# Splitting the first exponential of an attention step and the wide products beside it

## The chip, the cores and the metric

The kernel runs on one core of a Trainium2 chip. A core has five engines that run their own instruction streams and wait for each other through semaphores: TensorE (PE in the profile, with its weight loads shown apart as PEld), VectorE (DVE), ScalarE (ACT), GpSimd (POOL) and SyncE (SP), which here issues the DMA transfers. TensorE writes its results into PSUM, a memory of 128 partitions with eight banks of 512 fp32 columns each. VectorE and ScalarE read the results from there.

The metric is the time of one execution in device microseconds, as the median of several runs. One further execution is taken with the hardware profiler, and all the rows below come from it.

## The reference

The input is x of shape (8, 1024, 256): eight sequences of 1024 tokens. Sixteen heads of 16 columns each attend causally. Everything is fp32.

```python
mod = (_silu(c) @ wmod).reshape(8, 6, 1, -1)          # shift, scale and gate, twice
h = _layernorm(x) * (1 + ca) + sa
x = x + ga * attention(h)       # softmax(q k / 4, causal) v, 16 heads of 16, then w_out, b_out
h = _layernorm(x) * (1 + cb) + sb
# channel mix: xr, xk are mixtures of h and of h one token earlier
x = x + gb * sigmoid(xr @ W_r) * (relu(xk @ W_k) ** 2 @ W_v)
```

## The kernel before

**Units and steps.** Attention is done in 32 units, one for each of 8 sequences and 4 groups of 4 heads. A unit's 1024 queries are two chunks of 512 columns (`CW`), and its 1024 keys are eight tiles of 128. The table `STEPS` cuts a unit into nine steps, `a` to `e` for the tiles on the causal diagonal and `0` to `3` for the full tiles below it. Each step fills 512 columns of four banks with scores. Step `a` has one part of 512 columns, step `c` two of 256, and steps `b` and `d` have one of 128 and one of 384, because a diagonal tile needs only the queries from it on.

**What a step issues.** The function `step` is called once for each step of the whole program. It interleaves two kinds of work of two different units, nine steps apart (`LAG`):

- *Weights* (`weights`) of the older unit: for each of the four heads three rounds of products (`q,k` twice, for the high and low part of q, and `m,ones`, which subtracts the maximum) go into one bank. Then four exponentials on ScalarE, one for each head, read a whole bank each and write the tile `w`. Two heads make a half. GpSimd then zeroes what lies above the diagonal.
- *Maxima* (`maxima`) of the newer unit: two rounds of products (`k,q`) go into two pairs of banks, and VectorE takes the largest value of each row, for a diagonal tile with a mask added in place.

All eight banks are taken: four for the weights and four for the maxima. The rounds of a step lie in two streams. Stream 0 has the weights of half 0 and then the maxima of half 0. Stream 1 has the maxima of half 1 and then the weights of half 1. The loop at the end of `step` takes the next round from the stream that has had fewer columns so far (`took`), and the product's own column count is what is added. TensorE's order is fixed by this: each of its instructions is tied to the one before it (`InOrder` with `always`).

**What fills the rest of a step.** After the two streams come the *fills* that tables such as `POST` and `PREP` place on each step: the q and k projections (`qk`), the v projection and the output projection (`rows`), transposes (`transposed`), and the channel mix (`receptance`, `key`, `multiplied`). After two to three steps' worth of weights, `attend` multiplies the exponentials with v into a bank `po`, at the end of the step after the last one it needs. `attend` also reads `w` and so waits for GpSimd on the diagonal steps.

**Which bank a fill gets.** The functions `bank` and `banks_of_step` keep, for each bank, an estimated time at which it will be free, and hand out the one that is free first. For the first fill of a step this is in nearly all steps the bank of the step's first exponential.

**Strips.** Outside a few steps `by_strips` issues a product of 128 rows as four products of 32 output rows, one for each quarter of the array's columns, which run side by side. In `rows` the moving operand is 256 columns wide; in `qk`, `key` and `attend` it is as wide as the bank, 512 columns. Each fp32 product appears twice in the trace, as two passes.

**The end.** When no unit is left for the maxima, the flag `late[0]` is set and stays set for the last nine steps.

The profile puts every instruction at line 160, the helper that records it, so rows are told apart by the tiles they write and read. All PSUM banks are one tile named `banks`.

Of the kernel before, what the change touches and what calls it, by code (L numbers as in the profile page):

```python
# [10 lines left out]
AF = mybir.ActivationFunctionType  # L11
# [4 lines left out]
P = 128  # L16
B, N, D = 8, 1024, 256
H, HD = 16, 16
DC = D // P
CW = 512  # L20
NC = N // CW
NT = CW // P
HG = 4
NG = H // HG
ST = 32
# [28 lines left out]
FIRST, LAST = ("a", "f", "g"), ("e", "h", "i")  # L54
LAG = 9
BANKS = 8
PIECES = {0: NT, 1: 2 * NT}


# [15 lines left out]
def adaln_block(  # L75
# [24 lines left out]

    vacant, here = [0.0] * BANKS, [0.0]

# [35 lines left out]
    late = [False]  # L138
# [9 lines left out]
    start = [False]  # L148
# [28 lines left out]
    pe, dve, act = InOrder(nc.tensor, True), InOrder(nc.vector), InOrder(nc.scalar)  # L177
# [78 lines left out]
    wk_sb = load(w_k, D, "wk_sb")  # L256
# [54 lines left out]
    def v_tile(b, i):  # L311
        return v_of[(b * NC + i // NT) % (2 * NC)][:, i % NT]
# [121 lines left out]
    def by_strips(to, lhs, rhs, start, stop):  # L434


        if wide[0]:
            pe.matmul(to, lhs, rhs, start=start, stop=stop)
            return
        for j in range(P // ST):  # L440
            of = slice(j * ST, (j + 1) * ST)
            pe.matmul(to[of, :], lhs[:, of], rhs, start=start, stop=stop)
# [11 lines left out]
                )  # L454


    def prep(b, c):
        S = A[b, c]

        def stats(*ts):  # L460
            statistics(S["xa"], S, f"a{b}_{c}", ts)

        def norm(half):
            normalise(S["xa"], S, f"a{b}_{c}", half)
            if half == 0:
                return
            nxt = b * NC + c + 1
            if 1 < nxt < B * NC:
                later(lambda: load_xa(nxt // NC, nxt % NC))

        def turn():
            S["hT"] = sb.tile([P, DC, CW], F32, tag="hT", bufs=2, name=f"hT{b}_{c}")
            for d in range(DC):
                name = f"pta{b}_{c}_{d}"
                transposed(S["h"], S["hT"][:, d, :], b, d, SHIFT_A, SCALE_A, name)

        def qk(n, half):

            pq = bank(f"pq{b}_{c}_{n}_{half}")
            at = n * D + half * P  # L480
            for d in range(DC):
                by_strips(
                    pq, wqk_sb[:, d, at : at + P], S["hT"][:, d, :], d == 0, d == DC - 1
                )
            w, hi = (
                sb.tile([P, CW], F32, tag="qk", bufs=4, name=f"qk{b}_{c}_{n}_{half}{h}")
                for h in range(2)
            )
            if n == 0:
                act.mul(w, pq, SCALE)  # L490
            else:
                act.copy(w, pq)
            hi, lo = hi.bitcast(F32R), w.bitcast(F32R)
            pool.tensor_copy(hi, w)
            pool.tensor_sub(lo, w, hi.bitcast(F32))

            def away():
                to = (q_in, k_in)[n][b % 2][half]
                for h, of in enumerate((hi, lo)):
                    sync.dma_start(to[:, h, c * CW : (c + 1) * CW], of.bitcast(F32))  # L500

            later(away)

        def v(t0):
            pv = bank(f"pv{b}_{c}_{t0}")
            rows(pv, S["hT"], wv_sb, (t0, t0 + 1))
            to = v_of[(b * NC + c) % (2 * NC)]
            act.copy(
                to[:, t0 : t0 + 2, : H * (HD + 1)].rearrange(
                    "p t (h e) -> p t h e", e=HD + 1  # L510
                )[:, :, :, :HD],
                pv.rearrange("p (t h e) -> p t h e", t=2, e=HD),
            )

        return dict(
            stats0=lambda: stats(0, 1),
            stats1=lambda: stats(2, 3),
            stat0=lambda: stats(0),
            stat1=lambda: stats(1),
            stat2=lambda: stats(2),  # L520
            stat3=lambda: stats(3),
            norm0=lambda: norm(0),
            norm1=lambda: norm(1),
            turn=turn,
            q0=lambda: qk(0, 0),
            k0=lambda: qk(1, 0),
            q1=lambda: qk(0, 1),
            k1=lambda: qk(1, 1),
            v0=lambda: v(0),
            v2=lambda: v(2),  # L530
        )
# [127 lines left out]
    def weights(u, k, half, pws):  # L659

        diagonal = STEPS[k][0][2]
        V = U[u]
        qs, kk = qs_of[u % KEPT], k_of[u % KEPT]
        js = (2 * half, 2 * half + 1)
        pw = pws[half]
        parts, total = parts_of(k)
        rounds = []
        for c, kt, lo, cols in parts:
            for h in range(3):

                def products(c=c, kt=kt, lo=lo, cols=cols, h=h):
                    for n2, j in enumerate(js):
                        at = j * ST
                        if h < 2:
                            rs = slice(at, at + ST)
                            left = kk[rs, kt * P : (kt + 1) * P]
                            right = qs[h][rs, c * CW + lo : (c + 1) * CW]
                        else:
                            left = ones[at : at + 2, :]
                            right = V["m", c][at : at + 2, lo:]  # L680
                        pe.matmul(pw[n2][:, cols], left, right, start=h == 0, stop=h == 2)

                rounds.append((CW - lo, products))

        def exponentials():
            w = sb.tile([P, 2, CW], F32, tag="w", bufs=8, name=f"w{u}_{k}_{half}")
            for n2 in range(2):
                act.activation(w[:, n2, :total], pw[n2][:, :total], AF.Exp)
            if diagonal:

                blocks = len(parts)
                apart = parts[-1][3].start or CW
                on = w.rearrange("p h (m q) -> p h m q", q=apart)[:, :, :blocks, :P]
                pool.affine_select(
                    out=on,
                    in_=on,
                    pattern=[[0, 2], [0, blocks], [1, P]],
                    compare_op=ALU.is_ge,
                    fill=0.0,
                    base=0,  # L700
                    channel_multiplier=-1,
                )
            V["w", k, half] = w

        return rounds, exponentials, 0
# [4 lines left out]
    def attend(u, k, then):  # L710

        c, steps, _ = groups_of(u)[k]
        V = U[u]
        b, g = divmod(u, NG)
        po = bank(f"po{u}_{k}")

        parts = sorted(
            ((at, *part[1:]) for at in steps for part in parts_of(at)[0] if part[0] == c),
            key=lambda part: part[2],
        )  # L720
        ws = {(at, half): V["w", at, half] for at in steps for half in range(2)}
        for m, (at, kt, lo, cols) in enumerate(parts):
            for j in range(HG):
                pe.matmul(
                    po[j * ST : (j + 1) * ST, lo:],
                    v_tile(b, kt)[:, (g * HG + j) * (HD + 1) :][:, :ST],
                    ws[at, j // 2][:, j % 2, cols],
                    start=m == 0,
                    stop=m == len(parts) - 1,
                )  # L730
        then()
        if ("o", c) not in V:
            V["o", c] = sb.tile([P, CW], F32, tag="o", bufs=3, name=f"o{u}_{c}")
            act.copy(V["o", c], po)
        elif strict[0]:
            more = sb.tile([P, CW], F32, tag="more", bufs=2, name=f"more{u}_{k}")
            act.copy(more, po)
            pool.tensor_add(V["o", c], V["o", c], more)
        else:
            dve.tensor_add(V["o", c], V["o", c], po)  # L740
# [88 lines left out]
    def post(b, c):  # L829
        S = A[b, c]  # L830
# [75 lines left out]

        def key(e):
            pk = bank_apart(f"pk{b}_{c}_{e}")
            for d in range(DC):
                by_strips(  # L910
                    pk, wk_sb[:, d, e * P : (e + 1) * P], S["step"][:, d, :], d == 0, d == DC - 1
                )
            if e == 0:
                S["ka"] = sb.tile([P, DC, CW], F32, tag="mix", bufs=2, name=f"ka{b}_{c}")
            ka = S["ka"][:, e, :]
            act.activation(ka, pk, AF.Relu)
            pool.tensor_mul(ka, ka, ka)
# [204 lines left out]
    def step(T, T1, S, now, fill):  # L1122
# [26 lines left out]
        while any(lists):  # L1149
            s = min((s for s in range(2) if lists[s]), key=lambda s: (took[s], lists[s][0][3], s))  # L1150
            cols, products, after, _ = lists[s].pop(0)
            took[s] += cols
            products()
            if after:
                after()
# [290 lines left out]
```

## Time and profile before

| | |
|---|---|
| Median of three runs | 1377.53 us (1376.43 to 1382.0) |
| Profiled execution | 1386.23 us, with a span of 1384.5 us from the first to the last instruction |
| TensorE busy | 1284.9 us, 93% of the span |
| VectorE busy | 1056.9 us, 76% |
| ScalarE busy | 861.5 us, 62% |
| GpSimd busy | 710.7 us, 51% |
| DMA | 106 GB/s on average |
| Granted TensorE clock | 0.961 of full speed on average |

The profiled execution took 8.7 us more than the median of the unprofiled runs. Its busy shares are averages over some 300 steps that repeat the same pattern of nine. A matmul's end is modelled in the trace, so starts are the safer numbers on TensorE.

### The profile page before, as it was taken

The page shows a single profiled execution, that of the slowest core. Times are in us where ns is not written, and L with a number is a line of the kernel's source. Part 1 is how long each engine was busy: PE and PEld are TensorE (multiplying, and loading weights), DVE is VectorE, ACT ScalarE, POOL GpSimd, SP SyncE. Part 2 cuts the span into 40 slices and gives each one's busy share as a digit, 9 for nine tenths or more (in the row PEclk, how much of TensorE's full clock was granted, in tenths as well). Part 3 has the DMA queues.
Part 4 walks back from the last instruction along what each step waited for, and adds up shares of the span by engine and source line. Part 5 has one row for each costly group of instructions (what it writes and reads, how often), then busy time and mean ns, then how long its engine had stood idle before and what let it go on. Part 6 is the DMA issues. An engine that isn't in the chain of part 4 may idle for free.

```text
span 1384.5 us, 41749 instructions
## 1 busy us (share of the span) xinstructions
PE 1284.9 (93%) x16570; PEld 692.5 (50%) x16570; DVE 1056.9 (76%) x2910; ACT 861.5 (62%) x1679; POOL 710.7 (51%) x1088
## 2 busy tenths in 40 slices
PE   7898999999999899998999899998999989999988
PEld 4354555544455445554455454554455544544546
DVE  5776777788777877778777888778878788778745
ACT  2475677757567566765666666675666656656562
POOL 1334646546355556455565555564644556555352
PEclk8998999999999999999999999999999999999999
DMA  5114434422344323332434213443223323220111
GB/s 164 68 55 140 163 117 134 147 91 71 106 156 132 96 89 111 132 113 94 129 125 145 92 64 125 149 139 98 85 93 132 133 95 114 95 93 31 51 36 35
DMA packets 86515, 146.70 MB, mean 106 GB/s; under 512 B 12200, under 2 KB 42792, under 8 KB 86320
## 3 DMA queue, kind: packets, MB, share of 16 engines
q1 hardware_dynamic: 86112, 143.84, 31.4%
q8 instruction: 130, 2.13, 0.6%
q14 instruction: 65, 0.53, 0.1%
q10 hardware_dynamic: 208, 0.20, 0.0%
HBM read 86.35 MB, written 56.08 MB: 103 GB/s over the span
## 4 chain that ended last, share of the span: by engine, by line
PE 66%; DVE 9%; POOL 8%; ACT 7%; issue 5%; DMA 0%; POOLq 0%; DVEq 0%; ACTq 0%; SPq 0%
PE banks L160 66%; DVE mix L160 4%; ACT w L160 3%; DVE max L160 2%; POOL qk L160 2%; ACT w_e L160 1%; DVE banks L160 1%; POOL o L160 1%; POOL xb L160 1%; ACT w_d L160 1%; POOL oT L160 1%; POOL w_c L160 1%; POOL w_b L160 1%; POOL mrow L160 1%; POOL w_a L160 0%
## 5 line engine op out<-in xcount | busy, mean ns | idle before, releaser
L160 DVE CUSTOM_DVE_ANT_0 banks<-banks,mask 128x256 f32<-128x256 f32 (+3 forms) x1024 | 467.0, 525 | 121.9 <-PE banks L160 119.4
L160 PE MATMUL banks<-k,q 32*128 32x512 f32 (+3 forms) x3072 | 427.3, 371 | 5.8 <-DVE k L160 3.7
L160 PE MATMUL banks<-q,k 32*128 32x512 f32 (+3 forms) x3072 | 398.1, 369 | 5.4 <-ACT hT L160 1.2
L160 DVE TENSOR_REDUCE max<-banks 128x2 f32<-128x1024 f32 x256 | 302.5, 1221 | 91.7 <-PE banks L160 91.5
L160 PEld LDWEIGHTS banks<-q,k 32*128 32x128 f32 x3072 | 236.5, 185 | 149.0 <-ACT w L160 43.5
L160 ACT ACTIVATE w<-banks 128x512 f32<-128x512 f32 x512 | 264.2, 603 | 61.7 <-PE banks L160 58.4
L160 PE MATMUL banks<-m,ones 2*128 2x512 f32 (+3 forms) x1536 | 262.0, 351 | 8.7 <-DMA m<-mrow 8.7
L160 PEld LDWEIGHTS banks<-k,q 32*128 32x128 f32 x3072 | 252.0, 185 | 29.9 <-DVE max L160 5.9
L160 PEld LDWEIGHTS banks<-m,ones 2*128 2x128 f32 x1536 | 144.7, 185 | 16.1 <-DMA m<-mrow 7.1
L160 DVE DVE_READ_ACCUMULATOR2_ANT max<- 128x1 f32 x1024 | 143.2, 140 | 0.0
L160 PE MATMUL banks<-hT,wqk_sb 128*32 128x512 f32 x960 | 117.6, 610 | 10.6 <-ACT w_b L160 5.0
L160 PE MATMUL banks<-w,v 128*32 128x512 f32 x1024 | 123.2, 599 | 0.4 <-ACT w_a L160 0.2
L160 POOL TENSOR_TENSOR o<-o,more 128x512 f32<-128x512 f32 x62 | 79.2, 1277 | 69.0 <-ACT more L160 69.0
L160 PE MATMUL banks<-wr_sb,mix 128*32 128x256 f32 (+1 forms) x936 | 82.6, 502 | 27.9 <-DVE mix L160 27.7
L160 ACT ACTIVATE w_a<-banks 128x512 f32<-128x512 f32 x128 | 66.1, 602 | 36.3 <-PE banks L160 34.1
L160 POOL TENSOR_TENSOR qk<-qk,qk 128x512 fp32r<-128x512 f32 x60 | 81.0, 1350 | 5.0
L160 ACT ACTIVATE w_c<-banks 128x512 f32<-128x512 f32 x120 | 62.0, 602 | 24.7 <-PE banks L160 24.7
L160 DVE SCALAR_TENSOR_TENSOR mix<-step,mus,h2T 128x512 f32<-128x512 f32 x30 | 75.0, 2532 | 0.0
L160 POOL TENSOR_TENSOR xb<-xb,r 128x512 f32<-128x512 f32 x30 | 39.3, 1311 | 66.4 <-DVE r L160 55.6
L160 ACT ACTIVATE w_e<-banks 128x512 f32<-128x512 f32 x128 | 66.1, 604 | 10.0 <-PE banks L160 9.5
L160 ACT ACTIVATE w_d<-banks 128x512 f32<-128x512 f32 x120 | 62.0, 603 | 16.6 <-PE banks L160 14.6
L160 ACT ACTIVATE r<-banks 128x512 f32<-128x512 f32 x32 | 19.2, 600 | 84.8 <-PE banks L160 81.6
(166 smaller groups left out, 1993.6 us busy)
## 6 DMA issues: line engine op xcount, KB each, us to landing
q<-qin SPq DMA_DIRECT2D x60, 512.0 KB
qin<-qk SPq DMA_DIRECT2D x60, 256.0 KB
kin<-qk SPq DMA_DIRECT2D x60, 256.0 KB
k<-kin SPq DMA_DIRECT2D x30, 512.0 KB
od<-o SPq DMA_DIRECT2D x60, 256.0 KB
xa<-in_x SPq DMA_DIRECT2D x16, 512.0 KB
xb<-in_x SPq DMA_DIRECT2D x16, 512.0 KB
oT<-od SPq DMA_DIRECT2D x60, 128.0 KB
```

Source lines behind the costliest of these rows:

```text
L160: made = f(*args, **kwargs)
```

## The change

The change has four parts. The first concerns `exponentials`. In half 0 the first of the two exponentials is issued as two operations, over columns 0 to 255 and over the rest, unless `late[0]` is set. The second part is a new helper `columns`, which `qk` and `key` now call. It computes columns 0 to 255 of the bank completely, and then columns 256 to 511. The third part does the same for `attend`: all parts that reach into the first 256 columns, and then all parts for the last 256. The fourth part is in the loop that orders the rounds: a round of fewer than 256 columns now counts as 256. The number of columns multiplied and the choice of banks stay the same.

```diff
+SHORT = 256
...
+    def columns(to, lhs, rhs):
+
+        for of in (slice(0, CW // 2), slice(CW // 2, CW)):
+            for d in range(DC):
+                by_strips(to[:, of], lhs[:, d, :], rhs[:, d, of], d == 0, d == DC - 1)
+
...
             pq = bank(f"pq{b}_{c}_{n}_{half}")
             at = n * D + half * P
-            for d in range(DC):
-                by_strips(
-                    pq, wqk_sb[:, d, at : at + P], S["hT"][:, d, :], d == 0, d == DC - 1
-                )
+            columns(pq, wqk_sb[:, :, at : at + P], S["hT"])
...
             for n2 in range(2):
-                act.activation(w[:, n2, :total], pw[n2][:, :total], AF.Exp)
+
+                parted = half == 0 and n2 == 0 and not late[0]
+                for of in (
+                    (slice(0, CW // 2), slice(CW // 2, total)) if parted else (slice(0, total),)
+                ):
+                    act.activation(w[:, n2, of], pw[n2][:, of], AF.Exp)
...
-        for m, (at, kt, lo, cols) in enumerate(parts):
-            for j in range(HG):
-                pe.matmul(
-                    po[j * ST : (j + 1) * ST, lo:],
-                    v_tile(b, kt)[:, (g * HG + j) * (HD + 1) :][:, :ST],
-                    ws[at, j // 2][:, j % 2, cols],
-                    start=m == 0,
-                    stop=m == len(parts) - 1,
-                )
+        for first in range(0, CW, CW // 2):
+            here = [part for part in parts if part[2] < first + CW // 2]
+            for m, (at, kt, lo, cols) in enumerate(here):
+                of = slice(max(lo, first), first + CW // 2)
+                cols = slice(cols.start + of.start - lo, cols.start + of.stop - lo)
+                for j in range(HG):
+                    pe.matmul(
+                        po[j * ST : (j + 1) * ST, of],
+                        v_tile(b, kt)[:, (g * HG + j) * (HD + 1) :][:, :ST],
+                        ws[at, j // 2][:, j % 2, cols],
+                        start=m == 0,
+                        stop=m == len(here) - 1,
+                    )
...
             pk = bank_apart(f"pk{b}_{c}_{e}")
-            for d in range(DC):
-                by_strips(
-                    pk, wk_sb[:, d, e * P : (e + 1) * P], S["step"][:, d, :], d == 0, d == DC - 1
-                )
+            columns(pk, wk_sb[:, :, e * P : (e + 1) * P], S["step"])
...
             cols, products, after, _ = lists[s].pop(0)
-            took[s] += cols
+            took[s] += max(cols, SHORT)
```

## The prediction

> **What bounds the kernel now.** I read the page first: busy shares, clock, and the chain of work that ended last.
>
> ```profile
> span 1384.5 us, 41749 instructions
> PE 1284.9 (93%) x16570; PEld 692.5 (50%) x16570; DVE 1056.9 (76%) x2910; ACT 861.5 (62%) x1679; POOL 710.7 (51%) x1088
> ...
> PE 66%; DVE 9%; POOL 8%; ACT 7%; issue 5%; DMA 0%; POOLq 0%; DVEq 0%; ACTq 0%; SPq 0%
> ```
>
> TensorE holds two thirds of the chain, and the other engines come in between in short pieces. So TensorE's own order sets the pace, and what matters is what it stops for. The view of waits, for TensorE alone, tells that:
>
> ```profile
> PE banks L160 <- DVE mix L160: 27.7, 24, 2.1
> PE banks L160 <- ACT w L160: 8.9, 42, 0.3
> ...
> PE banks L160 <- ACT w_e L160: 6.1, 30, 0.3
> PE banks L160 <- ACT w_d L160: 5.8, 17, 0.4
> PE banks L160 <- ACT w_b L160: 5.4, 26, 0.3
> PE banks L160 <- ACT w_c L160: 3.2, 16, 0.3
> ```
>
> Apart from one wait on VectorE's `mix`, the frequent ones are all for ScalarE's exponentials. They look small because a product's modelled end hangs over the gap. The chain, cut to one step, shows the pattern that repeats:
>
> ```profile
> 1059.92 5.08 PE banks L160 x49
> 1065.00 0.59 ACT w L160
> 1065.59 0.04 issue
> 1065.63 6.54 PE banks L160 x68
> ```
>
> The same stretch in order of time, TensorE first and ScalarE next:
>
> ```profile
> 1065.11 0.39 PE L160 MATMUL banks<-k,q 32*128 32x512 f32 x1
> 1065.63 1.93 PE L160 MATMUL banks<-wob,oT 128*32 128x256 f32 x32
> 1067.50 0.50 PE L160 MATMUL banks<-q,k 32*128 32x512 f32 x2
> ...
> 1070.28 1.92 PE L160 MATMUL banks<-w,v 128*32 128x512 f32 x16
> ```
>
> ```profile
> 1064.98 2.07 ACT L160 ACTIVATE w<-banks 128x512 f32<-128x512 f32 x4 [0.27 <-PE banks L160]
> ```
>
> The last score product starts at 1065.11, and the fill could follow about 0.32 us later (where it waits for nothing, that is the distance behind a 512-column product). It starts at 1065.63 because it takes the bank of the first exponential, which began at 1064.98 and took 0.60 us. From the fill on TensorE runs without a stop into the next step's products.
>
> I compared all steps in the trace's records. Of 269 steps with four exponentials and a fill or `attend` behind them, 157 start it 53 ns after the first exponential's end. A further 57 are `attend` on the diagonal steps, which start 144 ns after it. Of these 214, 211 lie before the last nine steps. In 19 the fill starts 70 to 92 ns later than the first exponential would allow, and the rest wait for something else. So the end of the first exponential releases TensorE in 211 steps, and what moves this end moves the whole program.
>
> **Part 1: the exponential in two operations.** What a cut costs follows from ScalarE's rows of 512 and 384 columns:
>
> ```profile
> L160 ACT ACTIVATE w<-banks 128x512 f32<-128x512 f32 x512 | 264.2, 603 | 61.7 <-PE banks L160 58.4 <-issue 2.5 <-POOL mrow L160 0.4
> ...
> L160 ACT ACTIVATE w_h<-banks 128x384 f32<-128x384 f32 x8 | 3.3, 496 | 0.3 <-PE banks L160 0.2
> ```
>
> ```profile
> 1317.83 1.64 ACT L160 ACTIVATE w_h<-banks 128x384 f32<-128x384 f32 x4 [0.15 <-PE banks L160]
> ```
>
> Four of 512 columns take 2.07 us and the first 0.603, so each further one adds (2.07 - 0.603)/3 = 0.489. For 384 columns it is (1.64 - 0.495)/3 = 0.382. The slope is 0.107/128, or 0.84 ns a column. At 256 columns one alone takes about 0.603 - 0.214 = 0.389, and one behind another adds 0.275. The two halves end at 0.389 + 0.275 = 0.664: the first half is done 0.214 us earlier than now, the second 0.061 us later. Everything now depends on which end the fill waits for.
>
> Columns 0 to 255, which the fill writes first, are free after the first half. But the waits in the program of the kernel before are set by whole banks. Where VectorE reads columns 0 to 383 of a bank and then 384 to 511, and the next product writes only columns 0 to 127 or 0 to 255, that product waits for the later reading, which it does not touch, in all 79 such places. I take the same for ScalarE's readings. No exponential of the trace reads half a bank, so no row shows it. By whole banks the fill waits for the second half: 211 x 0.061 = 12.9 us. By columns it would start at the first half's end, or when the products end if that is later. Summed over the 214 steps, with the distance behind products of 512, 256, 384 and 128 columns at 316, 217, 258 and 200 ns, that is a gain of 25.5 + 11.4 = 36.9 us.
>
> [...]
>
> [...]
>
> The 19 fills with 70 to 92 ns of room lose nothing. The exponentials behind the first end 0.061 us later too, against TensorE, which is as late itself. The last one ends some 0.44 us before the next products in the single-fill steps, so nothing new waits there. GpSimd's zeroing of `w` moves with it. In some 15 steps TensorE waits for VectorE's `mix` (`receptance`), and one step's delay before that is absorbed: -0.9 us.
>
> **Parts 2 and 3: 256 columns for 512.** The timeline above has both: 32 products of 256 columns take 1.93 us, and 16 of 512 take 1.92, each one bank. In the records a set of four strips follows the last after 216 ns at 256 columns and 429 at 512, so two sets cost 3 ns more. The weight loads double, but at 256 columns they lie beside the products already. The trace has 960 + 432 + 1024 + 512 products of 512 columns in `qk`, `key` and `attend`, or 732 sets: 2.2 us. In `attend` on diagonals 120 sets of 384 columns become 128 + 256, at 109 + 216 ns for 322: 0.4 us. Together 2.6 us. From above, `wob,oT` has a mean of 234 per set where its median is 216; if all sets fell to that, 732 x 0.039 = 29 us. From below, nothing shortens: the distance from the last set to the next step's products is 522 ns behind 512 columns and 309 behind 256, just one set less.
>
> **Part 4: the order.** A short round costs about what 256 columns do: in the median of the records, rounds of 128 follow each other after 112 ns and rounds of 256 after 118. Four of nine steps are reordered (weights `b`, `c`, `d`, `0` against maxima `0`, `b`, `e`, `d`), some 124 in all, by one or two places; the order within each stream stays. TensorE works at the two streams on different rows of the array, and in the records a round starts ahead of one issued before it in the other stream. Stream 0's last weight round, which releases the first exponential, starts 789 ns into step `b`, set by its own stream. So I take 0. If a round got in the way or out of it in each, it would be 124 x 0.11 = 13.6 us either way. VectorE's `max` waits (2.6 us in all) are too small to make more of it. DMAs and GpSimd's queue are not moved.
>
> **Sum.** 12.9 + 2.6 - 0.9 = 14.6 us on the profiled execution's 1386.2, of which I keep 14 for the steps whose fill has a second reason to wait: 1400.2. The median of the runs before lies 8.7 us under the profiled one, so the median after is 1377.5 + 14 = 1391.5, rounded to 1391. The clock adds noise: in the trace it falls to half for 3.4 or 6.8 us some 20 times, mostly after the `mix` waits, and a shift in time can turn one into the other. At about 1.7 us each that is some 5 us either way.
>
> **The rivals.**
>
> *Release by columns (faster).* The fill starts at the first half's end. For it speaks that the fill needs only those columns first. Against it stand the 79 places of the program. 36.9 - 2.6 = 34 us less: 1343. At 36.9/214 = 0.17 us a step it would decide from some 63 steps on (63 x 0.17 = 10.9 us against 148 x 0.061 + 1.7 = 10.7 for the rest).
>
> *The delay is absorbed (same).* Another wait would have to lie right behind the exponential's end in more than half of the 211 steps. For it speaks that 57 start 144 ns late, perhaps with a second wait; against it that all 57 do so to within a few ns of the same distance. If those 57 lost nothing, 154 x 0.061 + 1.7 = 11 us remain, so absorption must reach the plain ones too. With a fifth of the 12.9 us left it would be 4 us: 1382.
>
> *Dearer narrow products (slower still).* All 732 sets at the mean of `wob,oT`: 14 + 26 = 40 us more, 1417. Against it: `wvb,ka`, `w_c,v` and `wv_sb,hT` have medians of 216 too.
>
> *The order matters.* 13.6 us either way on top: 1377 or 1405. Against it: the streams run side by side.
>
> **How the numbers follow.** The forecast has 0.74, release by columns 0.06, absorption 0.07, dearer products 0.05, the order 0.04 each way. 1391 is the likeliest case; its clock noise of 5 us and a cut between 46 and 76 ns (a quarter of 61 either way, 3.2 us) give 1383 to 1400 by themselves. The range takes in half of the order's reach on both sides: 1381 to 1402. A change under 0.5% (6.9 us) is what a measurement of this kernel hardly tells from none. Slower by more: the forecast but for 0.01, the dear products, the order's upper side and a little of the rest, 0.82. Within it: absorption and most of the order's lower side, 0.11. Faster: 0.07.
>
> **What would show it.** ScalarE has some 280 exponentials more, of 256 columns at about 390 ns. Fills start 53 ns after the end of the *second* half, and that is some 0.71 us behind the first one's start, where it was 0.65. Sets of 256 columns follow after 216 ns, and one bank still takes 1.92 us. TensorE's waits for `ACT w` grow. In the reordered steps the first exponential starts as far behind the step's first product as now (1.22, 1.10, 1.21 and 1.06 us). I would be wrong if fills began before the second half's end, or if the array lost more than 3 ns per pair of sets.

## The result and the profile after

The changed kernel takes 1392.89 us (median of 4 runs, 1389.32 to 1399.77), the kernel before, run beside it, 1376.98 us (1376.28 to 1382.0). The ratio is 1.0114 with a 95% interval of 1.0068 to 1.0159, so it is 9 to 22 us slower, and 15.9 us by the medians. Forecast were 1391 us and 14 us.

The page of the changed kernel, its span, busy shares and chain (of the chain's shares only the first five matter):

```profile
span 1390.9 us, 48983 instructions
...
PE 1279.3 (92%) x20022; PEld 803.0 (58%) x20022; DVE 1058.0 (76%) x2910; ACT 878.5 (63%) x1960; POOL 710.6 (51%) x1088
...
PE 69%; DVE 9%; ACT 8%; issue 6%; POOL 5%; DMA 0%; POOLq 0%; ACTq 0%; DVEq 0%; SPq 0%
```

ScalarE has 281 instructions more, TensorE 3452 records of products more, and still TensorE is busy no longer than before (1284.9 us). It is its stops that grew. The view of its waits (total, times and longest, in us):

```profile
PE banks L161 <- DVE mix L161: 25.0, 23, 2.0
PE banks L161 <- ACT w L161: 14.0, 57, 0.5
PE banks L161 <- ACT w_d L161: 9.8, 24, 0.4
PE banks L161 <- ACT w_b L161: 8.4, 30, 0.3
...
PE banks L161 <- ACT w_e L161: 7.9, 30, 0.3
PE banks L161 <- ACT w_c L161: 5.0, 15, 2.0
```

The five lines of `w` sum to 45.1 us, where they summed to 29.4 before. The 2.0 us at `w_c` is one wait that stood under `mix` before (27.7 there, 25.0 now). Without it the waits for exponentials grew by 13.7 us, nearly all of the loss.

One step of the chain, from a stretch that answers to the one shown of before:

```profile
1065.79 7.24 PE banks L161 x96
1073.03 0.05 ACT w L161
1073.08 0.22 issue
1073.30 0.39 ACT w L161
1073.68 0.04 issue
1073.73 3.58 PE banks L161 x49
```

And the same in order of time, TensorE first, then ScalarE (start, length, instruction):

```profile
1073.14 0.39 PE L161 MATMUL banks<-k,q 32*128 32x512 f32 x1
1073.73 1.93 PE L161 MATMUL banks<-wob,oT 128*32 128x256 f32 x32 [0.20 <-ACT w L161]
...
1078.43 1.93 PE L161 MATMUL banks<-w,v 128*32 128x256 f32 x32
```

```profile
1073.02 2.13 ACT L161 ACTIVATE w<-banks 128x256 f32<-128x256 f32 x5 [0.27 <-PE banks L161]
```

The five exponentials (two halves and three whole ones) take 2.13 us, where four took 2.07: the cut costs 0.06. The first half starts at 1073.02, the second 0.28 behind it at 1073.30, and it ends at 1073.68. The fill starts at 1073.73, 0.05 us behind the *second* half's end. Over the whole program the median fill starts 711 ns behind the start of the first exponential (651 before), and the `attend` of a diagonal step 803 ns (742 before). Measured from the end of the second half these are 53 and 144 ns, the same distances as from the end of the whole exponential before.

The groups of exponentials and of products, by shape (count, busy us and mean ns, idle time before them):

```profile
L161 ACT ACTIVATE w<-banks 128x256 f32<-128x256 f32 x248 | 81.7, 382 | 56.7 <-PE banks L161 53.5 <-issue 2.5 <-POOL mrow L161 0.4
```

```profile
L161 PE MATMUL banks<-w,v 128*32 128x256 f32 x2048 | 123.6, 382 | 0.9 <-ACT w_a L161 0.3 <-ACT w L161 0.2
L161 PE MATMUL banks<-hT,wqk_sb 128*32 128x256 f32 x1920 | 117.9, 387 | 13.3 <-ACT w_b L161 6.6 <-ACT w_e L161 3.4 <-ACT w_c L161 2.5
```

In the kernel before, the same two groups were:

```profile
L160 PE MATMUL banks<-w,v 128*32 128x512 f32 x1024 | 123.2, 599 | 0.4 <-ACT w_a L160 0.2
L160 PE MATMUL banks<-hT,wqk_sb 128*32 128x512 f32 x960 | 117.6, 610 | 10.6 <-ACT w_b L160 5.0 <-ACT w_e L160 2.6 <-ACT w_c L160 2.3
```

The narrow products cost nothing that shows here: 2048 of 256 columns take 123.6 us where 1024 of 512 took 123.2, and `qk` 117.9 where it took 117.6.

### The profile page after: what moved, and what is told of

Its sections match the earlier page's. It is cut to its first block, busy times and chain, and to the rows that moved or that the text cites. A ratio compares the mean times of both kernels' runs of the same rounds, so it can differ in the third digit from the quotient of the medians.

```text
span 1390.9 us, 48983 instructions
## 1 busy us (share of the span) xinstructions
PE 1279.3 (92%) x20022; PEld 803.0 (58%) x20022; DVE 1058.0 (76%) x2910; ACT 878.5 (63%) x1960; POOL 710.6 (51%) x1088
## 4 chain that ended last, share of the span: by engine, by line
PE 69%; DVE 9%; ACT 8%; issue 6%; POOL 5%; DMA 0%; POOLq 0%; ACTq 0%; DVEq 0%; SPq 0%
PE banks L161 69%; DVE mix L161 4%; DVE max L161 2%; ACT w_e L161 2%; ACT w L161 2%; POOL ka L161 1%; ACT w_a L161 1%; DVE banks L161 1%; ACT w_b L161 1%; POOL qk L161 1%; POOL o L161 1%; ACT w_d L161 0%; ACT ka L161 0%; POOL xb L161 0%; DMA m<-mrow 0%
## 5 line engine op out<-in xcount | busy, mean ns | idle before, releaser
L161 ACT ACTIVATE w<-banks 128x256 f32<-128x256 f32 (+1 forms) x636 | 272.1, 526 | 60.0 <-PE banks L161 56.8
L161 PE MATMUL banks<-hT,wqk_sb 128*32 128x256 f32 x1920 | 117.9, 387 | 13.3 <-ACT w_b L161 6.6
L161 PE MATMUL banks<-w,v 128*32 128x256 f32 x2048 | 123.6, 382 | 0.9 <-ACT w_a L161 0.3
L161 PE MATMUL banks<-wr_sb,mix 128*32 128x256 f32 (+1 forms) x936 | 76.3, 473 | 27.2 <-DVE mix L161 25.0
L161 PEld LDWEIGHTS banks<-hT,wqk_sb 128*32 128x32 f32 x1920 | 57.2, 111 | 62.7 <-ACT w_b L161 15.8
L161 PEld LDWEIGHTS banks<-w,v 128*32 128x32 f32 x2048 | 60.8, 109 | 52.1 <-ACT w L161 11.9
L161 ACT ACTIVATE w_a<-banks 128x512 f32<-128x512 f32 (+1 forms) x160 | 68.1, 523 | 35.8 <-PE banks L161 33.6
L161 ACT ACTIVATE w_c<-banks 128x512 f32<-128x512 f32 (+1 forms) x150 | 64.1, 522 | 21.9 <-PE banks L161 21.9
L161 ACT ACTIVATE w_d<-banks 128x512 f32<-128x512 f32 (+1 forms) x150 | 63.9, 524 | 17.3 <-PE banks L161 15.2
```

The costliest lines, as they stand in the source:

```text
L161: made = f(*args, **kwargs)
```

## The experiments

**How they are read.** The times of one kernel spread over 20 us: 29 runs of the kernel before gave 1366.5 to 1386.2. Nearly all of that is the granted clock, which falls to half for a while some 20 times in a run (22 times in the profiled execution of the kernel before, 20 in that of the changed one, where it has no value but full and half). Every run has its span S and its mean clock c, and the two parts can be separated. W = S x c is what the span would be at full clock, and H = 2 x S x (1 - c) is how long the clock was halved, so that S = W + H/2. In the trace of the kernel before, sets of four strips of 256 columns follow each other after 427 ns in the halved stretches and after 216 ns outside them, while ScalarE's exponentials of 512 columns take 597 and 602 ns. (A wait for another engine within a halved stretch is counted as if it were halved too, so W is a measure and no exact time.) Over 23 runs of the kernel before, W has a standard deviation of 1.2 us, and 0.8 to 2.0 us in the others. The mean over 4 to 12 runs is then good to 0.3 to 1 us (one standard error). For the profiled executions of the kernel before, the change and the experiment with the order alone, the cores' view says:

```profile
core 0: 1384.5 us, clock 0.961
```

```profile
core 0: 1390.9 us, clock 0.968
```

```profile
core 0: 1362.3 us, clock 0.977
```

That is W = 1330.5, 1346.4 and 1331.0. The first and third differ by 22 us in span and by half a microsecond of work.

| kernel | runs | median us | ratio to before, 95% | W | H |
|---|---|---|---|---|---|
| before, beside the first four | 23 | 1377.04 | | 1330.3 | 90.6 |
| before, beside the last four | 29 | 1376.53 | | 1330.6 | 87.5 |
| the whole change | 4 | 1392.89 | 1.0114 (1.0068 to 1.0159) | 1344.3 | 95.4 |
| cut alone | 6 | 1391.30 | 1.0107 (1.0055 to 1.0159) | 1343.5 | 93.2 |
| narrow products alone | 12 | 1376.50 | 1.0001 (0.9965 to 1.0037) | 1331.6 | 87.4 |
| order alone | 12 | 1369.95 | 0.9947 (0.9913 to 0.9980) | 1330.2 | 74.8 |
| cut in four | 4 | 1416.11 | 1.0288 (1.0230 to 1.0346) | 1370.0 | 89.9 |
| last exponential cut | 12 | 1381.90 | 1.0025 (0.9997 to 1.0054) | 1330.2 | 97.5 |
| whole change without the cut | 12 | 1382.98 | 1.0040 (1.0004 to 1.0077) | 1332.5 | 93.6 |
| order alone, steps longer | 12 | 1382.93 | 1.0034 (0.9999 to 1.0068) | 1335.4 | 90.7 |
| `receptance` one step later | 6 | 1405.66 | 1.0196 (1.0150 to 1.0242) | 1340.6 | 126.3 |

**The cut alone.**

```diff
-                act.activation(w[:, n2, :total], pw[n2][:, :total], AF.Exp)
+                parted = half == 0 and n2 == 0 and not late[0]
+                for of in (
+                    (slice(0, CW // 2), slice(CW // 2, total)) if parted else (slice(0, total),)
+                ):
+                    act.activation(w[:, n2, of], pw[n2][:, of], AF.Exp)
```

> Only the first exponential of a step is cut in two; products and order are those of before. Theory (the cut lies on the path: the fill waits for the whole bank, so for the second half): 211 steps x 0.061 us - 0.9 us = 12 us more than before, about 1389 us, with fills starting 0.71 us behind the first exponential's start instead of 0.65. Rival (the narrow products are what costs): no more than 2 us from before, 1377 to 1379. Rival (the order): the same as the second, 1377.

It gives the whole loss, as far as the uncertainty of W lets one tell: W rises by 13.2 us (14.0 in the whole change), the median by 14.3. Fills start 711 ns behind the first exponential and diagonal `attend`s 803, exactly as in the whole change.

**The narrow products alone.** (`columns` in `qk` and `key`, the two halves in `attend`.)

```diff
-            for d in range(DC):
-                by_strips(
-                    pq, wqk_sb[:, d, at : at + P], S["hT"][:, d, :], d == 0, d == DC - 1
-                )
+            columns(pq, wqk_sb[:, :, at : at + P], S["hT"])
...
+        for first in range(0, CW, CW // 2):
+            here = [part for part in parts if part[2] < first + CW // 2]
```

> Only the products of qk, key and attend are 256 columns wide; the exponential is whole and the order is that of before. Theory (the cut is the cost): 2.6 us more than before, about 1379.5 us, with 216 ns between sets of 256 columns. Rival (the narrow products cost): most of the 14 us measured for the whole change, 1387 to 1393.

W rises by 1.3 us, half of the 2.6 expected, and the interval of the ratio reaches 0.4% to either side of 1. Fills start 651 and 742 ns behind the first exponential, as before: the narrow products don't move what releases TensorE.

**The order alone.**

```diff
-            took[s] += cols
+            took[s] += max(cols, SHORT)
```

> Only the order of the rounds changes: a short round counts as 256 columns. Theory: 0 to 1 us less than before, since in the changed kernel the first exponential of step c starts 36 ns earlier (1067 for 1103 ns behind the first product) in 30 steps and the other steps stay: 1376 to 1377 us. Rival (the order costs): up to 13 us more, 1390. Rival (the order hides part of the cost): 5 us less or more of a gain, 1372 or below.

The expected time was missed: the kernel is 7 us faster than before, with an interval that leaves out no change. W is 1330.2, a difference of -0.1. The whole gain is H, which falls from 90.6 to 74.8 us, and half of 15.8 is 7.9. It is the fastest kernel of the study, faster than the one before and the changed one. Where it loses less shows in the windows (the window and its length in us; busy us and instructions of TensorE's products, its loads, VectorE, ScalarE and GpSimd; then the granted clock, the DMA share and GB/s). First the kernel before, around one `mix`, which VectorE begins at 295.76 us:

```profile
294.00:300.00 6.00, 3.84 (x64) 1.92 (x56) 6.00 (x4) 4.61 (x9) 5.84 (x9) 0.98 0.42 143
300.00:306.00 6.00, 5.40 (x52) 2.25 (x56) 6.00 (x20) 0.60 (x1) 2.72 (x3) 0.50 0.91 253
306.00:312.00 6.00, 5.65 (x96) 3.38 (x92) 4.27 (x14) 3.05 (x6) 2.44 (x5) 0.95 0.09 30
```

Then the order alone, at the same `mix`, which begins at 291.96 us:

```profile
294.00:300.00 6.00, 3.08 (x42) 1.32 (x38) 6.00 (x13) 1.89 (x4) 4.87 (x5) 0.80 0.95 248
300.00:306.00 6.00, 5.65 (x88) 3.09 (x84) 5.90 (x22) 3.26 (x6) 1.88 (x5) 0.92 0.40 143
306.00:312.00 6.00, 5.80 (x80) 2.71 (x72) 4.79 (x24) 4.10 (x8) 1.92 (x4) 1.00 0.15 51
```

Before, the clock is halved for 6 x 2 x (0.02 + 0.50 + 0.05) = 6.8 us, with the order alone for 6 x 2 x (0.20 + 0.08) = 3.4 us. The group of the `receptance` products that wait for `mix` shows the same over the program, first of the kernel before, then of the order alone:

```profile
L160 PE MATMUL banks<-wr_sb,mix 128*32 128x256 f32 x928 | 79.5, 502 | 27.9 <-DVE mix L160 27.7 <-ACT w L160 0.2
```

```profile
L161 PE MATMUL banks<-wr_sb,mix 128*32 128x256 f32 x928 | 67.2, 439 | 28.0 <-DVE mix L161 27.8 <-ACT w L161 0.2
```

They wait as long (27.7 and 27.8 us), but the same 928 products run at a mean of 439 ns instead of 502. (These are one execution each, 1386 us near the slow end of its kernel's runs and 1364 us near the fast end, so they differ by more than the means do.)

**The first exponential in four.** If fills wait for the last piece, four pieces cost about three times what two do; if they wait only for the columns they write, four are better than two.

```diff
-                act.activation(w[:, n2, :total], pw[n2][:, :total], AF.Exp)
+                for of in (
+                    [slice(q, min(q + P, total)) for q in range(0, total, P)]
+                    if parted
+                    else (slice(0, total),)
+                ):
+                    act.activation(w[:, n2, of], pw[n2][:, of], AF.Exp)
```

> As the run with the cut alone, but the first exponential is cut into four operations of 128 columns (three cuts for one). Theory: the cost goes with the number of cuts. From the rows of 512 and 384 columns a cut adds 61 ns, so three add 183 ns in 211 steps and some 100 ns in the 19 with little room: 38.6 + 2 = 40 us more than before, about 1417 us. Rival (any cost is a fixed one of a second wait or of a changed phase of the clock, not of the cut itself): the same as with one cut, about 1389 us.

W rises by 39.7 us, as expected from whole banks. ScalarE and TensorE in one step of it:

```profile
1090.70 2.26 ACT L160 ACTIVATE w<-banks 128x128 f32<-128x128 f32 x7 [0.27 <-PE banks L160]
```

```profile
1090.82 0.39 PE L160 MATMUL banks<-k,q 32*128 32x512 f32 x1
1091.54 1.93 PE L160 MATMUL banks<-wob,oT 128*32 128x256 f32 x32 [0.33 <-ACT w L160]
```

The seven exponentials take 2.26 us (0.19 more than four), and the fill starts 0.84 us behind the first. Four pieces end 0.19 us later than one, and the fill starts 0.19 us later, again some 53 ns behind the end of the last piece; 211 x 0.19 = 40 us.

**The last exponential of the step instead.** It has the same 281 operations more on ScalarE, but nothing on TensorE waits for that end.

```diff
-                act.activation(w[:, n2, :total], pw[n2][:, :total], AF.Exp)
+                parted = half == 1 and n2 == 1 and not late[0]
+                for of in (
+                    (slice(0, CW // 2), slice(CW // 2, total)) if parted else (slice(0, total),)
+                ):
+                    act.activation(w[:, n2, of], pw[n2][:, of], AF.Exp)
```

> As the run with the cut alone, but the last exponential of a step is cut (half 1, second head) in place of the first: the same number of operations, another place. Theory (the cut costs because the fill waits for the first exponential's bank): the last one ends 0.44 us ahead of the next step's products, so nothing moves: 1376 to 1379 us, and the span times the mean granted clock stays at 1330 us. Rival (ScalarE's own load costs, wherever the cut is): 12 to 14 us more, 1390 us and 1343.

W is 1330.2, within 0.4 us of the kernel before. The median is 5 us higher and lies above what was expected, by H (97.5 against 87.5). A step of it, ScalarE and then TensorE:

```profile
1065.56 2.13 ACT L160 ACTIVATE w<-banks 128x512 f32<-128x512 f32 x5 [0.27 <-PE banks L160]
```

```profile
1065.61 0.46 PE L160 MATMUL banks<-k,q 32*128 32x512 f32 x2
1066.21 1.93 PE L160 MATMUL banks<-wob,oT 128*32 128x256 f32 x32
```

The five exponentials take 2.13 us as in the changed kernel, but the fill starts 0.65 us behind the first one, as before. So the cut costs TensorE nothing by its load on ScalarE; it costs only where its end releases a bank.

**The whole change without the cut.**

```diff
-                parted = half == 0 and n2 == 0 and not late[0]
-                for of in (
-                    (slice(0, CW // 2), slice(CW // 2, total)) if parted else (slice(0, total),)
-                ):
-                    act.activation(w[:, n2, of], pw[n2][:, of], AF.Exp)
+                act.activation(w[:, n2, :total], pw[n2][:, :total], AF.Exp)
```

> The changed kernel with the first exponential whole again: narrow products and the new order stay. Theory: the cut was all of the cost; span times mean clock 1330.3 + 1.3 - 0.1 = 1331.5 us, so 13 less than the changed kernel's 1344.3, and a time of 1370 to 1379 us, by how often the clock falls to half. Rival (narrow products and order cost together with the cut): 1385 us or more.

W is 1332.5. From here the cut adds 11.8 us to reach the changed kernel, where it added 13.2 to the kernel before. The median again came out above the expectation, by H: the 15.8 us that the order alone took off H are not there once the narrow products are added.

**The order alone, with the steps made a little longer.** To see whether the gain of the order lies in the order or in where its waits fall against the clock, the transposition of the maxima is done twice in every step.

```diff
-            took[s] += cols
+            took[s] += max(cols, SHORT)
...
-        pe.transpose(of, V["max"][:, c], ident)
+        for _ in range(2):
+            pe.transpose(of, V["max"][:, c], ident)
```

> The order alone, and the transposition of the maxima issued twice (the second writes the same values again), 64 times some 0.1 us more on TensorE. It shifts the steps of a sequence by 0.8 to 0.9 us against the grid of 3.41 us on which the clock changes. Theory (the 7 us that the order alone gained is a matter of when its waits fall on that grid: span times clock was 1330.2 for 1330.3, but 74.8 us at half clock for 90.6): span times clock goes to 1337, and the time at half clock goes back up to 88, give or take 8, for a total of about 1383 us. Rival (the order shortens what makes the clock fall): the time at half clock stays at 75 and the total is 1377 us.

W rises by 5 us over the order alone, but the median by 13, since H goes back from 74.8 to 90.7. The order is the same, and its gain is gone.

**`receptance` one step later.** In the trace of the kernel before, 11 of the 22 halved stretches begin in a wait for `mix` or in the fill behind it. This places the projection that waits one step later in the kernel before, so that VectorE is done by then.

```diff
-    18 x.turn; 18 x.mix; 19 x.mixed00; 19 x.mixed01; 20 x.receptance0; 20 x.receptance2;
+    18 x.turn; 18 x.mix; 19 x.mixed00; 19 x.mixed01; 21 x.receptance0; 21 x.receptance2;
...
-    28 y.mixed01; 29 y.receptance0; 29 y.receptance2; 29 y.mixed10; 29 y.mixed11; 31 y.key0;
+    28 y.mixed01; 30 y.receptance0; 30 y.receptance2; 29 y.mixed10; 29 y.mixed11; 31 y.key0;
```

> The kernel before with one thing moved: the products of receptance are placed one step later (21 for 20, and 30 for 29), so that VectorE's mix is done when TensorE comes to them. Theory (the waits for mix, 1.1 to 2.3 us in 12 steps, are what makes the clock fall to half): both go, the waits' 12 x 1.5 = 18 us or a large part of it, and some 40 to 50 of the 90 us at half clock, worth 20 to 25 us: 1335 to 1350 us. Rival (the wait moves to another product, key, or the clock falls for another reason): 1370 us or more, with 80 us or more at half clock.

The expectation failed: the time rises by 29 us, about 10 of it in W and the rest through H. The waits for `mix` are gone from the list, but another stands in their place (TensorE's waits):

```profile
PE banks L160 <- DVE max L160: 42.9, 16, 4.9
```

VectorE around such a place:

```profile
291.64 2.36 DVE L160 TENSOR_REDUCE max<-banks 128x2 f32<-128x1024 f32 x2 [1.39 <-PE banks L160]
293.92 5.86 DVE L160 SCALAR_TENSOR_TENSOR mix<-step,mus,h2T 128x512 f32<-128x512 f32 x2
299.70 0.55 DVE L160 CUSTOM_DVE_ANT_0 banks<-banks,mask 128x384 f32<-128x384 f32 x1
```

The readings of the maxima stand behind the two `mix` operations, 5.86 us, in VectorE's queue. Without `receptance` to fill that time TensorE runs into the next maxima's banks and waits up to 4.9 us instead of 2.1, and H rises to 126.3 us. The wait comes from VectorE's queue, and placing `receptance` later does not remove it.

## Why the prediction was right, step by step

*TensorE's order sets the pace, and the first exponential's end releases it in 211 steps.* Right, and in a few more. Cutting the first exponential costs 13.2 us (11.8 on the other parts), cutting the last one, with the same work on ScalarE, -0.4 us. The price follows the fill's delay: 60 ns cost 13 us, 190 ns cost 39.7.

*Release by whole banks, not by columns.* Right, and the step that decided the sign. The fill starts 53 ns behind the second half's end, and with four pieces behind the last of them. By columns the cut would have gained some 37 us, by the forecast's own estimate. What the runs show is where the program waits. No run here let TensorE write one part of a bank while ScalarE read another: a form with the wait for the first half only was not tried.

*The cut costs 0.061 us.* Right: 0.060 and 0.061 by the starts of the fills. A half takes 383 ns (estimated 389) and the second starts 280 ns behind the first. 211 x 0.060 = 12.7 us, against W's 13.2 and 11.8.

*The 19 fills with 70 to 92 ns of room lose nothing.* Wrong for 12 of them, at a small price. These are all products of the channel mix (`wvb,ka`). In the kernel before they start 741 to 744 ns behind the first exponential's start, 144 ns behind its end, just as the diagonal `attend`s do. With the cut alone and in the whole change they start at 802 to 804, and with four pieces at 930. So they had no room, but wait for the same end. With them it is 223 steps, and 223 x 0.060 = 13.4 us.

*The `mix` waits absorb 0.9 us of it.* Too small to be told: 27.7 us of waits became 27.0 in the two traces, a difference within the uncertainty of W.

*Narrow products, 2.6 us.* The mechanism was right, the size twice what the work measured: +1.3 us alone, with an uncertainty of about half a microsecond. Sets of 256 columns follow each other after 216 ns in `qk`, `key` and `attend`, and a bank still takes 1.93 us. The forecast counted 3 ns for each of 732 sets as if all stood on the path. The rival with 234 ns for a set (26 us more) is out.

*The order, 0.* Right for the work (-0.1 us), wrong for the time. The 13.6 us on either side were argued from rounds that get in each other's way. No such effect was found: in the changed kernel the first exponential starts 1.22, 1.21 and 1.05 us into the steps `b`, `d` and `0`, and 1.07 in `c` (1.10 before). What the order alone did, 7 us, it did through the clock.

*Clock noise, 5 us either way.* Too small a term, and here luck came in. It was worked out as chance from run to run, and it put the falls mostly behind the `mix` waits, where 11 of the 22 are. The runs of one kernel do spread by 10 us either way, but the mean shifts as well: between kernels with W within 0.4 us of each other, H goes from 74.8 to 97.5 us, 11 us of time. In the whole change it came out at 95.4 against 90.6, 2.4 us, so the sum held: 14.0 us of W and 2.4 of clock make 16.4, and the medians say 15.9. Forecast by its terms were 12 for the cut, 2.6 for the products and 0 for the order. Measured alone they are 13.2, 1.3 and -0.1, 14.4 together, so the parts add up. The mechanism of the cut was foreseen. That the total came within 2 us was luck in two ways: the cut was taken too small and the narrow products too dear by about as much, and the clock's mean moved little. With the H of the order alone (74.8) the same W would have given about 1383 us.

*The delay is absorbed.* Out. The diagonal `attend`s, which start 144 ns behind the exponential and might have had a second wait, moved by 61 ns with the rest.

## What to carry to other kernels

Before a producer or a reader is cut in pieces so that its bank comes free earlier, find out whether waits go by bank or by columns: if by bank, each cut only adds its fixed price (here 60 ns) to the end that releases, times the number of steps in which that end is what the bottleneck waits for. Where the clock changes within a run, compare span times mean clock beside the times: here it resolves about 1 us where the times spread by 20, and it told less work from a better clock.

## What had not been expected of the hardware

The halved clock is not noise but has a grid. In nine of the ten profiled executions each stretch within the span lasts 3.41 or 6.83 us and starts within 3 ns of a grid of 3.413 us. In the run with `receptance` later one lasts 10.24. Fitted to the starts alone, the interval of the grid is 3413.3 ns in the trace of the kernel before (22 stretches, each within 0.5 ns of it) and the same in the changed kernel's (20 stretches, within 0.6). At the fills that wait for `mix` the clock falls in or behind waits of 0.8 to 2.15 us (3.1 together with the second wait of the same fill, at most).

What a wait costs depends on where it falls in the grid. A `receptance` fill that waits for `mix` takes 4.44 us from its first product to its last at full clock, and up to 7.16 us where a halved stretch falls in it. There are 12 such fills in each of the nine executions, 108 in all (the tenth has none). This is when the next grid point came after the end of a fill's first wait, and what followed:

| next grid point, us after the wait's end | fills | halved stretch |
|---|---|---|
| 0.01 to 0.29 | 17 | 3.41 us in 14, 6.83 in 3 |
| 0.35 to 0.72 | 20 | 6.83 us in all |
| 0.83 to 2.46 | 42 | 3.41 us in all |
| 2.48 to 2.71 | 9 | none |
| 2.88 to 3.40 | 20 | none in 11; in 9 one that had begun up to 0.54 us before the wait's end |

So the place tells what follows in 71 of the 108 fills without an exception, and at both ends of the interval it leaves it open. Why the clock falls so is not shown.

In the profiled executions this is also where the order's gain lies. With the order alone, five of the six fills called `y` in the tables lie at 2.91 to 3.16 and have no stretch; before, only one of all 12 had none. With the steps made longer three of these `y` fills lie at 0.87 to 0.91 and have 3.41 us, and of the `x` fills, which lay at 0.57 to 1.25, three lie at 0.27 to 0.38 and have 6.83. With the order alone the waits of `x` end 160.5 to 160.7 us apart but for one (163.4), which is 47.0 to 47.1 intervals of the grid, so the place hardly moves from sequence to sequence. Before, they end 161.8 to 164.5 us apart, 47.4 to 48.2 intervals, and it wanders. Part of these times is the halved stretches themselves. So the 7 us of the order alone are real for that kernel, but they are no property of the order, and a further change of the period may take them away: the three other kernels here that have this order have an H of 90.7 to 95.4.
